# A fused attention and expert block on one Trainium2 core: set-up, the last batch's gathers and the experts' gathers put in another order

## The chip, the cores and the metric

The kernel runs on one core of a Trainium2 chip. A core has five engines, each with its own queue: TensorE (PE, matrix products into PSUM), VectorE (DVE), ScalarE (ACT), GpSimd (POOL) and SyncE (SP, which here only issues DMAs). They wait for each other by semaphores. The metric is the device time of one execution in microseconds; lower is better. All arithmetic is in float32.

## The reference, cut to what matters

```python
mod = (silu(c) @ wmod).reshape(16, 6, 1, 256)
sa, ca, ga, sb, cb, gb = six rows of mod         # ga, gb kept away from zero
h = layernorm(x) * (1 + ca) + sa                 # x is 16 x 1024 x 256
x = x + ga * attention(h)                        # layernorm, q k v, rope, 16 heads of 16,
                                                 # causal softmax, out projection, + h
h = layernorm(x) * (1 + cb) + sb
x = x + gb * experts(h)                          # 8 experts, each gathers 512 rows by index,
                                                 # 256 -> 1024 gelu -> 256, weights, scatter-add
```

The indices are drawn at random, so that one row can belong to several experts, or twice to one.

## The kernel before, in words

**Set-up.** The modulation is computed and written to DRAM, tables of rope are turned, and batch 0 is taken up to its q, k and v. `steps_h` (L428) makes the pieces of the two norms of one half of a batch: statistics `x0` to `x3`, `x moments`, `x power`, `x norm`, `scale`, `shift`, then the same for `h`: statistics (L440, VectorE), `h moments` (L445, VectorE), `h power` (L450 to L454, GpSimd), `bias` (L495, GpSimd, which adds the row `bo_bc`), `h norm` (L465, ScalarE), `gate` and `onto` (GpSimd). In set-up `h_of(2, ...)` issues pieces of batch 1's first half, `h_of(0, ...)` and `h_of(1, ...)` those of batch 0.

`output_bias` (L335) adds the layer norm's offset to v's bias, scales `wv_sb`, and multiplies the bias by Wo into the PSUM tile `pbo` (L352). It returns a function, `joins`, that adds `pbo` to `bo_bc` on VectorE (L359).

**Maxima.** For each group of four heads `maxima` (L622) makes ten steps, each with a product of q and k for every head (L640, into one of six PSUM buffers of the pool `ps_s`) and a minimum of the negated, masked product on VectorE (L658 or L662). The four heads lie in four groups of 32 rows of the array. The first group of batch 0 is done in set-up by `own(n)`: four products, then four minima. Behind step n the loop issues `step_v` of token block n - 1 (L573): a product `pv` in the one buffer of the tag `misc`, and ScalarE's copy into `v_pad` (L583).

**Attention.** A batch has four groups of ten steps; a step issues scores `s` (L717), the exponential on ScalarE (L730), GpSimd's triangular mask on diagonal blocks (L735, steps 0, 1, 2, 5, 7 and 9), the products `o` with v (L764) of the step before, and the maxima of the group that follows. Lists name what else each step issues: `pieces` (products), `inside` (VectorE) and `extra` (the rest), all in program order. In the last batch, `extra` holds twenty gathers of modulation rows for experts 0 and 1 (`rows_mod`, L187, issued in L100); output rows of batch 2 are projected (L856), copied by ScalarE (L869) and added to x by GpSimd (`y`, L876), in steps 2 and 4 of groups 1 and 2.

**Experts.** The attended rows lie in DRAM in `rows` and `out`. For expert e: rows are gathered (`rows_x`, tile `xg`), VectorE takes their statistics (`stats`, L1220, L1222), GpSimd the inverse deviation (`powers`, L1226, L1227), VectorE norms and modulates them (`hidden`, L1235 to L1241), TensorE turns them (`turned`, L1250) and makes `ph` (`first`, L1261, with ScalarE's gelu in L1264), `often` (VectorE) counts rows that occur more than once, and `second` makes `fo` (L1286, two PSUM buffers), weighs it (L1289, L1290), adds the current row of `out` (L1294, tile `cur`, gathered by `rows_now`), and scatters the sum back (L1296). Since rows repeat, a scatter waits for the scatter before it, and the gathers of `cur` for the last scatter of the expert before.

**Order.** TensorE, VectorE, ScalarE and GpSimd issue in program order throughout, SP too in set-up; in the rest a scheduler places SP's DMAs. GpSimd issues every gather and scatter, each in one instruction, between its other work.

Of the kernel before, what the change touches and what calls it, by code (L numbers as in the profile page):

```python
# [11 lines left out]
F32 = mybir.dt.float32  # L12
# [4 lines left out]
ALU = mybir.AluOpType  # L17
AX = mybir.AxisListType

P = 128  # L20
# [7 lines left out]
def adaln_block_kernel(  # L28
# [27 lines left out]
    nc = tc.nc  # L56

    B, L, D = x.shape
# [139 lines left out]
    with ExitStack() as actx:  # L198
# [136 lines left out]
        def output_bias():  # L335

            pv = ps_s.tile([P, QC], F32, name="pb_v", tag="s")[:, :KC]
            for j in range(KC):
                for k in range(KC):
                    nc.tensor.matmul(  # L340
                        pv[:, j : j + 1],
                        lhsT=wv_sb[:, k, ts(j, P)],
                        rhs=bet[:, k : k + 1],
                        start=(k == 0),
                        stop=(k == KC - 1),
                    )
            nc.vector.tensor_tensor(bvc, pv, bvc, ALU.add)
            for k in range(KC):
                nc.vector.tensor_scalar(wv_sb[:, k, :], wv_sb[:, k, :], gam[:, k : k + 1], None, ALU.mult)
            pbo = ps_s.tile([P, QC], F32, name="pbo", tag="s")[:, :D]  # L350
            for k in range(KC):
                nc.tensor.matmul(  # L352
                    pbo,
                    lhsT=bvc[:, k : k + 1].to_broadcast([P, P]),
                    rhs=wo_rows[:, k, :],
                    start=(k == 0),
                    stop=(k == KC - 1),
                )
            return lambda: nc.vector.tensor_tensor(bo_bc, pbo, bo_bc, ALU.add)  # L359

        def indices():
            nc.vector.tensor_single_scalar(bidx, idx, shift, ALU.arith_shift_right)
# [578 lines left out]
        def do(items):  # L941
            for item in items:
                (item[1] if isinstance(item, tuple) else item)()

        with tc.manual_schedule(engines=ORDERED | {ET.SP}):
            nc.sync.dma_start(out=c_sb, in_=cT.rearrange("(k p) b -> p k b", p=P))
            load_wm(0)
            load_x(0)
            raw = [spare("rot00", f"raw{n}").rearrange("p (k n) -> p k n", k=KC) for n in range(2)]
            tabs = [  # L950
                spare("rot01", f"tab{n}")[:, : NT * DH].rearrange("p (t d) -> p t d", d=DH) for n in range(2)
            ]
            for n, src in enumerate((rope_cos, rope_sin)):
                nc.scalar.dma_start(out=tabs[n], in_=src)
            for n, src in enumerate((Wq, Wk)):
                nc.scalar.dma_start(out=raw[n], in_=src.rearrange("(k p) n -> p k n", p=P))
            nc.scalar.activation(sg, c_sb, AF.Sigmoid)
            constants()
            for n, src in enumerate((bq, bk)):
                nc.sync.dma_start(out=bcol[:, n, :], in_=src.rearrange("(p e) -> p e", e=2))  # L960
            nc.sync.dma_start(out=gam, in_=ln_gamma)
            nc.sync.dma_start(out=bet, in_=ln_beta)
            load_x(1)
            load_wm(1)
            nc.sync.dma_start(out=wv_sb, in_=Wv.rearrange("(k p) n -> p k n", p=P))
            nc.sync.dma_start(out=idx, in_=top_idx.rearrange("(t p) e -> p t e", p=P))

            for a in range(2):
                for g in range(GH):
                    to = slice(W * g + DH * a, W * g + DH * (a + 1))  # L970
                    at_ = dict(a=2, g=GH, d=DH)
                    nc.sync.dma_start(out=wo_sb[to], in_=Wo.rearrange("(k a g d) n -> a g d k n", **at_)[a, g])
            wo_rows = spare("rot11", "wo_rows").rearrange("p (k n) -> p k n", k=KC)
            nc.sync.dma_start(out=wo_rows, in_=Wo.rearrange("(k p) n -> p k n", p=P))
            nc.sync.dma_start(out=bvc, in_=bv.rearrange("(k p) -> p k", p=P))
            nc.sync.dma_start(out=bo_bc, in_=bo.partition_broadcast(P))
            nc.vector.tensor_mul(sg, sg, c_sb)
            first_rows()
            hs = [steps_h(0, half) for half in range(NC)] + [steps_h(1, 0)]
            turns, turned, rots, vs = prep[0]  # L980

            def h_of(n, *names):
                for name in names:
                    hs[n].pop(name)()


            for half in range(NC):
                tables(half)
                h_of(half, "x0", "x1", "x2", "x3", "x moments", "x power")
            copies = modulation_products(0)  # L990
            for n in range(2):
                for e in range(2):
                    for k in range(KC):
                        nc.vector.tensor_scalar(
                            wqk[:, k, n, e, :], raw[n][:, k, e::2], gam[:, k : k + 1], None, ALU.mult
                        )
            input_bias()
            ones()
            h_of(0, "x norm0", "x norm1")
            h_of(1, "x norm0", "x norm1")  # L1000
            do(copies)
            copies = modulation_products(1)
            h_of(0, "scale0", "scale1", "shift0", "shift1", "h0", "h1", "h2", "h3", "h moments", "h power")
            do(copies)
            h_of(1, "scale0", "scale1")
            h_of(1, "shift0", "shift1", "h0", "h1", "h2", "h3", "h moments", "h power")
            h_of(0, "h norm0", "h norm1")
            do(turns[0])
            modulation(0)
            load_mod(0)  # L1010
            load_mod(1)
            modulation(1)
            h_of(1, "h norm0", "h norm1")
            indices()

            do(turned[0][:4] + rots[0][:1])
            h_of(2, "x0", "x1", "x2", "x3", "x moments", "x power")
            do(turned[0][4:])
            do(turns[1])
            tokens()  # L1020
            joins = output_bias()
            h_of(2, "x norm0", "x norm1")
            do(rots[0][1:])
            operands(0, 0, 0)
            h_of(2, "scale0", "scale1", "shift0")
            do(turned[1][:4] + rots[1][:1])
            h_of(2, "shift1")
            do(turned[1][4:] + rots[1][1:])
            operands(0, 0, 1)
            h_of(2, "h0", "h1", "h2", "h3", "h moments", "h power")  # L1030
            joins()
            units, place = maxima(0, 0)

            def own(n):
                product, rest = units[n]
                tiles = [product(h) for h in range(GH)]
                for h in range(GH):
                    rest(h, tiles[h])

            for n in range(NS):  # L1040
                own(n)
                do(vs[n - 1 : n] if n else [])
                if n == 0:
                    operands(0, 1)
                    h_of(2, "bias0", "bias1", "h norm0", "h norm1")
                if n == mid:
                    place(0)
                if n == mid + 3:
                    h_of(2, "gate0", "gate1", "onto0", "onto1")
                    for half in range(NC):  # L1050
                        h_of(half, "bias0", "bias1", "gate0", "gate1", "onto0", "onto1")
            do(prep[1][0][0])
            place(1)
            load(2)
            assert not any(hs), [h.keys() for h in hs]
        actx.enter_context(tc.manual_schedule(engines=ORDERED))
        for b in range(B):
# [16 lines left out]
            if b + 1 == B:  # L1074
# [1 line left out]
                    each(pw, w[8 * c + 8 : 8 * c + 12])  # L1076
                at(2, [lambda: weights_1(0), first_mod, early_mod])
                at(2 * NS + mid + 4, [lambda: weights_2(0)])
                for n in range(5):
                    for t_ in range(NCT):  # L1080
                        at(NS + n * NCT + t_, [lambda n=n, t_=t_: rows_mod(t_)[n]()])
                at(3 * NS, [gated[b]])
                each(proj[b][0], [at0 + 3 * NS + mid + n for n in range(3, 7)])
            elif b > 0:
# [220 lines left out]

    nc.scalar.activation(fc.tile([P, 1], F32, name="table"), eps[:, 0:1], AF.Gelu_apprx_tanh)

    def later_mod(e):

        m = fw.tile([P, NCT, 3 * D], F32, name=f"modg_{e}", tag="modg", bufs=3)  # L1310
        for t in range(NCT):
            gather(m[:, t, :], mod_c[:, :], bidx[:, t, e : e + 1])
        X[e]["shift"], X[e]["scale"] = m[:, :, 0:D], m[:, :, D : 2 * D]
        X[e]["gate"] = lambda t: m[:, t, 2 * D : 3 * D]

    halves = ALL[: NCT // 2], ALL[NCT // 2 :]
    for at in halves:
        stats(0, at)
        powers(0, at)
        rows_x(1, range(1) if at[0] == 0 else range(1, NCT))  # L1320
    for at in halves:
        hidden(0, at)
        turned(0, at)

# [14 lines left out]
    for e in range(E):  # L1339
# [5 lines left out]
            turned(e + 1)  # L1345
        if e + 2 < E:
            stats(e + 2)
            later_mod(e + 2)
        if e > 0:
            rows_now(e)  # L1350
        if e + 2 < E:
            powers(e + 2)
        if e + 3 < E:
            rows_x(e + 3)
# [74 lines left out]
```

## Time and profile before

| | us |
|---|---|
| median of three runs | 2824.04 (2823.45 to 2824.58) |
| the profiled execution, its own time | 2825.22 |
| its span, first to last instruction | 2823.5 |
| set-up, until the first maxima are done on TensorE | about 76 |
| attention | about 2490 |
| experts | about 255 |

| stretch, us | TensorE busy | VectorE | ScalarE | GpSimd | granted clock |
|---|---|---|---|---|---|
| 0 to 36 | 25.48 | 31.82 | 14.80 | 18.28 | 0.91 |
| 36 to 76 | 37.14 | 33.74 | 8.34 | 38.03 | 0.87 |
| 76 to 2412 | 2334.29 | 1831.72 | 1478.76 | 1331.14 | 1.00 |
| 2412 to 2564 | 146.94 | 88.66 | 92.62 | 69.59 | 1.00 |
| 2564 to 2597 | 18.05 | 16.29 | 6.47 | 20.04 | 0.74 |
| 2597 to 2819 | 214.57 | 115.53 | 38.84 | 105.62 | 0.99 |

Times in the profile are microseconds from the start of the span. A row of an order of time reads: start, duration, engine, line, operation, output<-input, and in brackets how long the engine was idle before it and what ended that. "Granted clock" is the share of TensorE's full clock in the stretch. A product is shown until its modelled end, so a busy TensorE isn't TensorE at its best rate.

### The profile page before, as it was taken

The numbers are of one execution on the slowest core, as the hardware profiler recorded it, in microseconds if no ns is written. First come the engines' busy times: TensorE is split into PE (matmuls) and PEld (weight loads), VectorE is DVE, ScalarE is ACT, GpSimd is POOL, SyncE is SP. The second block draws the span as 40 slices with busy tenths as digits, with TensorE's granted clock in tenths as the row PEclk, the third lists the DMA queues.
The fourth block names the chain that finished last, engine by engine and source line by source line (L and its number), as shares of the span: only waits on it lengthen the run. The fifth ranks groups of instructions, "written<-read, shape, count | busy, mean of one in ns | idle before, by whom it ended". The sixth has DMA issues, their size and how long they took to land.

```text
span 2823.5 us, 63046 instructions
## 1 busy us (share of the span) xinstructions
PE 2776.5 (98%) x22409; PEld 1274.6 (45%) x22409; DVE 2117.8 (75%) x6759; ACT 1639.8 (58%) x3342; POOL 1582.7 (56%) x2187
## 2 busy tenths in 40 slices
PE   8999999999999999999999999999999999997998
PEld 5444444444444444444444444444444444444665
DVE  8887878787878778787878777787878777754554
ACT  3566666666666666666666666666666665662211
POOL 7565655546564655556464646555554666354552
PEclk8999999999999999999999999999999999998999
DMA  4211222212122222222121222222222222124551
GB/s 143 65 45 41 57 54 68 64 51 73 52 62 60 67 60 56 55 69 64 51 71 52 61 64 66 53 58 62 69 62 54 67 48 66 49 78 163 175 198 54
DMA packets 200314, 199.84 MB, mean 71 GB/s; under 512 B 93248, under 2 KB 154368, under 8 KB 200000
## 3 DMA queue, kind: packets, MB, share of 16 engines
q1 hardware_dynamic: 173888, 148.35, 19.7%
q0 software_dynamic: 8448, 24.78, 2.7%
q10 hardware_dynamic: 17664, 22.68, 2.6%
q8 instruction: 177, 2.90, 0.4%
q14 instruction: 137, 1.12, 0.1%
HBM read 118.94 MB, written 75.66 MB: 69 GB/s over the span
## 4 chain that ended last, share of the span: by engine, by line
PE 94%; POOL 1%; DVE 1%; issue 1%; DMA 1%; ACT 0%; POOLq 0%; SPq 0%; DVEq 0%; ACTq 0%
PE s L717 41%; PE o L764 21%; PE pqk L545 9%; PE m L640 6%; PE pv L576 5%; PE pw L856 5%; PE ph L1261 3%; PE fo L1286 3%; PE ptx L526 1%; DMA cur<-out_dram,idx 0%; POOL modg L100 0%; DMA xg<-rows,idx 0%; DVE wide L311 0%; PE fpt L1250 0%; POOL r L495 0%
## 5 line engine op out<-in xcount | busy, mean ns | idle before, releaser
L730 ACT ACTIVATE p<-s 128x512 f32<-128x512 f32 (+1 forms) x2560 | 1279.5, 552 | 882.1 <-PE m L640 814.4
L640 PE MATMUL m<-ko,qo 32*128 32x512 f32 (+3 forms) x6144 | 1407.4, 526 | 1.7 <-DVE bo_bc L359 1.5
L717 PE MATMUL s<-qo,ko 32*128 32x512 f32 (+3 forms) x6144 | 1351.9, 524 | 0.4 <-DMA qo<-max 0.4
L735 POOL TENSOR_SCALAR_AFFINE_SELECT p<-p 128x256 f32<-128x256 f32 x1024 | 417.7, 416 | 937.2 <-ACT p L730 934.2
L658 DVE TENSOR_REDUCE mt<-m 128x1 f32<-128x512 f32 x1024 | 669.6, 685 | 209.3 <-PE m L640 188.4
L717 PEld LDWEIGHTS s<-qo,ko 32*128 32x128 f32 x6144 | 513.0, 183 | 594.4 <-issue 423.9
L764 PE MATMUL o<-p,v_pad 128*32 128x256 f32 (+3 forms) x6848 | 651.4, 463 | 3.2 <-POOL p L735 2.9
L662 DVE CUSTOM_DVE_ANT_0 masked<-m,dmask,mt 128x256 f32<-128x256 f32 (+3 forms) x1024 | 515.3, 546 | 130.3 <-PE m L640 129.2
L662 DVE CUSTOM_DVE_ANT_0 masked<-m,dmask 128x512 f32<-128x512 f32 (+3 forms) x1024 | 454.9, 486 | 194.6 <-PE m L640 170.8
L640 PEld LDWEIGHTS m<-ko,qo 32*128 32x128 f32 x6144 | 561.8, 183 | 10.0 <-DVE mt L662 3.1
L764 PEld LDWEIGHTS o<-p,v_pad 128*32 128x32 f32 x6848 | 149.1, 108 | 427.1 <-issue 173.9
L545 PE MATMUL pqk<-xnT,wqk 128*128 128x256 f32 x1024 | 286.6, 405 | 0.9 <-ACT xnT L527 0.9
L545 PEld LDWEIGHTS pqk<-xnT,wqk 128*128 128x128 f32 x1024 | 175.2, 189 | 190.8 <-issue 148.3
L479 POOL TENSOR_TENSOR h<-h,mod 128x512 f32<-128x512 f32 x120 | 152.7, 1274 | 67.7 <-ACT h L465 64.4
L662 DVE DVE_READ_ACCUMULATOR2_ANT mt<- 128x1 f32 x2048 | 169.7, 83 | 0.0
L576 PE MATMUL pv<-wv_sb,xnT 128*128 128x256 f32 x512 | 146.6, 409 | 0.3 <-ACT v_pad L583 0.3
L1264 ACT ACTIVATE gT<-ph,b_sb 128x512 f32<-128x512 f32 x64 | 43.9, 687 | 177.2 <-PE ph L1261 171.6
L856 PE MATMUL pw<-wo,onT 128*128 128x256 f32 x512 | 144.2, 405 | 0.6 <-DVE onT L813 0.6
L576 PEld LDWEIGHTS pv<-wv_sb,xnT 128*128 128x128 f32 x512 | 87.7, 191 | 97.7 <-issue 68.7
L552 DVE SCALAR_TENSOR_TENSOR rot<-pqk,bcol,cosT 128x256 f32<-128x256 f32 x256 | 122.0, 477 | 8.0 <-PE pqk L545 3.8
L856 PEld LDWEIGHTS pw<-wo,onT 128*128 128x128 f32 x512 | 86.9, 189 | 89.3 <-issue 70.9
L552 DVE SCALAR_TENSOR_TENSOR rot<-pqk,bcol,sinT 128x256 f32<-128x256 f32 x256 | 121.3, 474 | 0.0
(136 smaller groups left out, 2236.3 us busy)
## 6 DMA issues: line engine op xcount, KB each, us to landing
ops<-rot SPq DMA_DIRECT2D x128, 256.0 KB
rec<-rec_d SPq DMA_DIRECT2D x504, 32.0 KB
rows<-y SPq DMA_DIRECT2D x62, 256.0 KB
out_dram<-y SPq DMA_DIRECT2D x62, 256.0 KB
w<-in_W_dram SPq DMA_DIRECT2D x14, 1024.0 KB
qo<-ops SPq DMA_DIRECT2D x192, 64.0 KB
ko<-ops SPq DMA_DIRECT2D x192, 64.0 KB
x<-in_x_dram ACTq DMA_DIRECT2D x24, 512.0 KB
```

The lines of the kernel that those rows point to most:

```text
L479: nc.gpsimd.tensor_tensor(h, h, row(n), op)
L545: nc.tensor.matmul(ps, lhsT=wqk[:, k, n, e, :], rhs=xt[:, k, ts(u, QW)], start=(k == 0), stop=(k == KC - 1))
L552: nc.vector.scalar_tensor_tensor(s["rot", half, n, e, f][:, ts(u, QW)], ps, bcol[:, n, e : e + 1], tab[:, half * QC + u * QW : half * QC + ...
L576: nc.tensor.matmul(pv, lhsT=S[b]["xnT", t // TC][:, k, ts(t % TC, P)], rhs=wv_sb[:, k, :], start=(k == 0), stop=(k == KC - 1),)
L640: nc.tensor.matmul(sc[:, sum(w[:n]) : sum(w[: n + 1])], lhsT=q[rows, ts(i, P)], rhs=k[rows, c * QC : c * QC + w[n]], start=True, stop=True,)
L658: nc.vector.tensor_reduce(dst, sc[:, 0:w], AX.X, ALU.max, negate=True)
L662: nc.vector.tensor_tensor_reduce(out=masked[:, 0:w], in0=sc[:, 0:w], in1=dmask[:, QC - w : QC], scale=-1.0, scalar=mt[half][:, 0, h, i % T ...
L717: nc.tensor.matmul(sc[:, o:e], lhsT=k[rows, ts(j_, P)], rhs=q[rows, c_ * QC + q0 : (c_ + 1) * QC], start=True, stop=True,)
L730: nc.scalar.activation(p[:, h, 0:end], sc[:, 0:end], AF.Exp, scale=scale)
L735: nc.gpsimd.affine_select(out=mine, in_=mine, compare_op=ALU.is_ge, fill=0.0, base=0, pattern=[[0, 3 - n], [0, n], [1, P]], channel_multip ...
L764: nc.tensor.matmul(acc[c][W * g : W * (g + 1), q0:q1], lhsT=v[:, j, h * VW + 1 - DH * (G % 2) : h * VW + 1 - DH * (G % 2) + W], rhs=p[:, g ...
L856: nc.tensor.matmul(po, lhsT=s["onT", c][:, k, ts(t, P)], rhs=s["wo"][:, k, :], start=(k == 0), stop=(k == KC - 1),)
```

## The change

It moves instructions; it adds and removes none.

1. `pbo` and its addition to `bo_bc` become `product_bias`, issued behind step 0 of the maxima. Before, the product stood in `output_bias`, the addition ahead of step 0.
2. The statistics, moments and power of batch 1's `h` move from ahead of step 0 to behind step 2; so do its bias and norm, which stood behind step 0.
3. In `own(n)` the product of v stands between the products of heads 0, 1 and those of heads 2, 3, ahead of the minima.
4. The twenty gathers of `rows_mod` go into steps 3, 6 and 7 of group 0 (two each) and steps 2, 3, 6 and 7 of groups 1 and 2 (one, two, two, two) instead of one in each step of groups 1 and 2.
5. In the loop over experts, the modulation rows of token blocks 0 and 1 are gathered ahead of the current rows, those of blocks 2 and 3 behind them; before, all four stood ahead.
6. In the first expert, `hidden` and `turned` of the first half of the rows come before `stats` of the second half.

```diff
+        def product_bias():
             pbo = ps_s.tile([P, QC], F32, name="pbo", tag="s")[:, :D]
...
-            return lambda: nc.vector.tensor_tensor(bo_bc, pbo, bo_bc, ALU.add)
+            nc.vector.tensor_tensor(bo_bc, pbo, bo_bc, ALU.add)
...
-            joins = output_bias()
+            output_bias()
...
-            h_of(2, "h0", "h1", "h2", "h3", "h moments", "h power")
-            joins()
             units, place = maxima(0, 0)
 
             def own(n):
                 product, rest = units[n]
-                tiles = [product(h) for h in range(GH)]
+                tiles = [product(h) for h in range(GH // 2)]
+                do(vs[n - 1 : n] if n else [])
+                tiles += [product(h) for h in range(GH // 2, GH)]
                 for h in range(GH):
                     rest(h, tiles[h])
 
             for n in range(NS):
                 own(n)
-                do(vs[n - 1 : n] if n else [])
                 if n == 0:
+                    product_bias()
                     operands(0, 1)
+                if n == mid - 1:
+                    h_of(2, "h0", "h1", "h2", "h3", "h moments", "h power")
                     h_of(2, "bias0", "bias1", "h norm0", "h norm1")
...
-                for n in range(5):
-                    for t_ in range(NCT):
-                        at(NS + n * NCT + t_, [lambda n=n, t_=t_: rows_mod(t_)[n]()])
+
+                free = steps([(3, 3, 6, 6, 7, 7), (2, 3, 3, 6, 6, 7, 7), (2, 3, 3, 6, 6, 7, 7)])
+                for i, n in enumerate(free):
+                    at(n, [lambda i=i: rows_mod(i % NCT)[i // NCT]()])
...
-    def later_mod(e):
-
-        m = fw.tile([P, NCT, 3 * D], F32, name=f"modg_{e}", tag="modg", bufs=3)
-        for t in range(NCT):
+    def later_mod(e, at):
+
+        if at[0] == 0:
+            X[e]["mod"] = fw.tile([P, NCT, 3 * D], F32, name=f"modg_{e}", tag="modg", bufs=3)
+        m = X[e]["mod"]
+        for t in at:
             gather(m[:, t, :], mod_c[:, :], bidx[:, t, e : e + 1])
...
         rows_x(1, range(1) if at[0] == 0 else range(1, NCT))
-    for at in halves:
         hidden(0, at)
         turned(0, at)
...
         if e + 2 < E:
             stats(e + 2)
-            later_mod(e + 2)
+            later_mod(e + 2, halves[0])
         if e > 0:
             rows_now(e)
         if e + 2 < E:
+            later_mod(e + 2, halves[1])
             powers(e + 2)
```

## The prediction

> **What bounds the kernel now.** I read the engines' shares first, then the chain that ended last, then TensorE's waits.
>
> ```profile
> PE 2776.5 (98%) x22409; PEld 1274.6 (45%) x22409; DVE 2117.8 (75%) x6759; ACT 1639.8 (58%) x3342; POOL 1582.7 (56%) x2187
> ...
> PE 94%; POOL 1%; DVE 1%; issue 1%; DMA 1%; ACT 0%; POOLq 0%; SPq 0%; DVEq 0%; ACTq 0%
> ```
>
> TensorE is the bound over attention, whose order the diff leaves alone. The edits can only touch the places where TensorE stands idle or slow. Its waits (total, times, longest) name them:
>
> ```profile
> PE fpt L1250 <- issue: 13.6, 1, 13.6
> PE o L764 <- POOL p L735: 2.9, 4, 1.6
> PE fo L1286 <- DVE fy L1289: 2.4, 1, 2.4
> PE m L640 <- DVE bo_bc L359: 1.5, 1, 1.5
> PE fo L1286 <- DVE fy L1294: 0.9, 1, 0.9
> ```
>
> A wait can cost more than itself. The stretches of set-up show the granted clock (the share before "DMA share"):
>
> ```profile
> 47.00:50.00 3.00, 1.54 (x13) 1.15 (x10) 2.40 (x11) 0.00 (x0) 3.00 (x4) 1.00 0.65 175
> 50.00:54.00 4.00, 4.00 (x15) 3.41 (x16) 4.00 (x21) 0.00 (x0) 3.77 (x6) 0.52 0.56 153
> 54.00:57.00 3.00, 2.73 (x12) 0.93 (x11) 1.13 (x9) 2.44 (x5) 3.00 (x4) 0.50 0.25 77
> 57.00:60.00 3.00, 3.00 (x12) 1.41 (x12) 1.47 (x8) 0.38 (x1) 3.00 (x3) 0.50 0.40 101
> ```
>
> After the 1.46 us wait TensorE ran at half clock from 50 to 60, and VectorE stood idle for 1.9 and 2.2 us there.
>
> GpSimd's order of time at a group boundary of the last batch, and VectorE's in two experts:
>
> ```profile
> 2508.34 1.28 POOL L876 TENSOR_TENSOR y<-y,x 128x512 f32<-128x512 f32 x1 [5.78 <-ACT y L869]
> 2509.77 0.96 POOL L100 DMA_INDIRECT gate<-mod_g,bidx  x1
> 2510.75 1.28 POOL L832 TENSOR_TENSOR part<-oT,rec 128x512 f32<-128x512 f32 x1
> 2512.11 1.27 POOL L835 TENSOR_TENSOR onT<-onT,part 128x512 f32<-128x512 f32 x1
> 2513.33 1.51 POOL L735 TENSOR_SCALAR_AFFINE_SELECT p<-p 128x256 f32<-128x256 f32 x4
> ```
>
> ```profile
> 2721.60 0.43 DVE L1294 TENSOR_TENSOR fy<-fy,cur 128x256 f32<-128x256 f32 x1 [5.98 <-DMA cur<-out_dram,idx]
> ...
> 2752.72 0.42 DVE L1294 TENSOR_TENSOR fy<-fy,cur 128x256 f32<-128x256 f32 x1 [7.54 <-DMA cur<-out_dram,idx]
> ```
>
> First, a gather stands between GpSimd's late `y` and the masks that `o` waits for. Second, VectorE waits 5.98 and 7.54 us for current rows.
>
> **The Trainium skill.** "TensorE: Matmul & The Clock Gate", Part 1: the array falls to half rate after about one idle window of 3.4 us, which runs free, and returns after a busy one. The trace agrees on the size (half clock in multiples of about 3.4 us), but a 1.46 us wait was enough. Same page, specification table: only weight loads are pulled ahead; ScalarE, VectorE and GpSimd are strict FIFO. So one product waiting for its PSUM buffer holds all behind it: the trace has this at 50.0. "DMA: Bandwidth & Descriptors", Anatomy of one DMA: about 2 us fixed, mostly the receipt; here a scatter of rows takes 2.41.
>
> **Set-up.** The statistics of batch 1's `h` (L440, L445) and the sum into `bo_bc` leave VectorE's queue ahead of the maxima; `pbo` moves behind the first step; the v projections stand between heads 0,1 and 2,3. SP's order is unchanged.
>
> *Gain.* Without `pbo` (1.10) ahead of pqk, VectorE's wait of 1.58 at 40.43 goes and its rotations end at about 45.75 instead of 47.35. But the first maxima products need q and k loads, issued on SP at 41.86 to 45.97 behind GpSimd's rotation of 38.39 to 41.2, which does not move; so they stay at 46.7 to 47.5. VectorE starts on them at 47.2 instead of 49.86. The split of heads costs TensorE nothing: heads 2,3 of one step run beside heads 0,1 of the next (two passes of 0.53), so a step needs 1.06 plus 1.06 for pv, under VectorE's 2.4 to 2.7.
>
> *New wait.* VectorE: step 0 is 4 x 0.61 to 49.65, `bo_bc` 0.3, step 1 4 x 0.56 and step 2 4 x 0.48 to about 55.3 (with short waits for products), then statistics 4 x 0.36 and 0.34: 57.1. Before, they ended at 49.6. GpSimd, idle from 51.0, starts its power then (1.86, from 50.98 to 52.84): 59.0; two biases of 1.23: 61.4; ScalarE's norm of the second half 1.1: about 62.6; and only then, in its queue, the copy of the third pv (0.37): 63.0. The fourth pv has one PSUM buffer and waits for that copy, and the products of step 4 and on stand behind it. TensorE reaches it near 56.7. It idles 6.4 us, where before the like wait was 0.27 (at 56.73). VectorE eats its six tiles by 60.8 and idles too. From pv3 on, VectorE has 1.2 + 2.7 + 2.4 + 2.7 + 2.4 + 2.15 from about 65, to 78.9; TensorE ends 2.4 ahead of it, at 76.5 instead of 75.5: 1.0 lost. Half clock after 6.4 idle holds for 3.4 to 6.8 us of work, half of that lost: 1.7 to 3.4, say 2.5. TensorE also idles 44.6 to 46.65 before the first products; one slow window there delays step 0 and `pbo` by about 1.3. Sum: 4.8 lost, between 1.0 (no slow clock) and 6.5. GpSimd's remaining 16 operations of 1.23 end at 81 to 82.5 instead of 74.9; the first mask stands 4.2 behind TensorE's end (79.76 against 75.52), so near 84.5: covered, but by 2 only.
>
> **Gathers of the last batch.** Twenty gathers (0.95 and 0.30 of issue each) move from one a step to free steps without masks. At the boundaries of groups 1 and 2 none stands behind the late `y` any more; masks come 0.96 + 0.15 = 1.1 earlier, twice: 2.2 gained (at 2474.99 `o` took 1.70 instead of 0.64 with a wait of 0.25, so there is that much to gain at each). In the new places: after step 3's none, GpSimd then waits for `rec` until 2431.6; after steps 6 and 7 of group 0, 2.5 us each inside idle stretches of 4.89 and 1.06 + 2.10; the last pushes `onT` (2446.45) to 2447.8, done before its mask at 2449.82. Cost nothing, 0.7 to spare. Range 1.5 to 2.7.
>
> **Experts.** Two of four modulation gathers (1.26 each) go behind the four of the current rows. Current rows are asked for 2.5 earlier and queue behind half the modulation's bytes. TensorE has two `fo` buffers of 3.45 us each, so VectorE may wait about 5.1 before TensorE does: 5.98 gave 0.87, 7.54 gave 2.43. Against this, at 2710.72 and 2740.29 the last scatter was issued just as a weight load of 1 MB began (SP, 2710.34 and 2739.90); scatters issued so late in other experts held the next for 5.4 to 6.5 instead of 3.2. So the gather may start not 2.5 but 1 to 2 earlier; it then finds an emptier queue, lands in about 2.5 to 3 instead of 4.5 and 6.0, and VectorE's waits become about 3. Both TensorE waits go, 3.3, and the slow clock after the second (16 products in 5.37 instead of 3.47): 1.9. Sum 5.2, between 3.3 and 5.5. GpSimd's later half of the modulation is needed an expert later: hidden.
>
> **First expert.** `hidden` of the first half (0.70 + 0.69 + 0.74) now precedes the second half's statistics. The first starts 1.1 earlier (2573.55 against 2574.68), but nothing uses it alone. The second: statistics from 2575.7, VectorE done at 2576.7, GpSimd's power to 2577.9, `hidden` to 2580.2 instead of 2579.04. All hidden rows are needed for `ph` (2580.32), and ScalarE's eight DMA issues to 2585.26 start behind the copies, so `ph` and its activation come 1.1 later: 1.25 lost with the slow clock, 0 to 2.
>
> **Sum** on the profiled execution (span 2823.5; own time 2825.22, 1.2 above the median 2824.04): +4.8 - 2.2 - 5.2 + 1.25 = -1.35. The median becomes 2822.7.
>
> **Rivals.** (1) The set-up's stall meets no slow clock, as the free window allows: 1.0 instead of 4.8, in all -5.2: 2818.9. For: before had phases of full clock beside waits of 0.9. Against: 6.4 idle is near two windows. (2) Slower: in experts 4 and 5 the current rows' gather waits for the last scatter, held by the weights until they are in, as issues 2738 on suggest. If it lands later than 5.1 after VectorE is ready, TensorE still waits and the 5.2 shrink to nothing: +3.9, 2827.9. For: the coincidence within 0.4 us in both experts. Against: once the scatter lands, only two modulation gathers are ahead. (3) The norm's detour is hidden after all, and set-up wins what VectorE stops idling, 3.7: 2814.2. Against: ScalarE's order is fixed.
>
> **Numbers.** Forecast 0.50 (alone 2820 to 2825.5), rival 1 0.22, rival 2 0.20, rival 3 0.05, worse 0.03. Leaving a tenth at each side and adding the bounds: 2818.0 to 2828.2. A change of 0.2% is 5.65 us, about what a measurement can tell: faster takes rival 3 and a third of rival 1, 0.12; slower the tail of rival 2 and worse, 0.06; within 0.82.
>
> **What would show it.** A TensorE wait of some 6 us at `pv` for ScalarE's `v_pad` near 57 to 63, slow clock after; no wait at `fo`; `o` at group boundaries without gather ahead; VectorE's `cur` waits under 5; `ph` of the first expert about 1 later. Wrong if pv does not wait, or `fo` still does.

## The result, and the profile after

The changed kernel takes 2830.47 us (median of 14 runs, 2825.33 to 2836.7) against 2822.93 (14 runs, 2819.03 to 2824.69): 1.0029 times the time, 95% interval 1.0022 to 1.0036. It is slower by 7.5 us by the medians. The forecast was 2822.7, and 2828.2 its upper end. The profiled execution has a span of 2829.1 us (its own time 2831.12), 5.6 more than the one before. The profiles hold less of the loss than the medians, since the profiled execution of before lay 2.3 above the median of its 14 runs, that of after 0.7.

TensorE is still the bound. From the page of the kernel after, its engines and its chain:

```profile
PE 2778.5 (98%) x22409; PEld 1276.1 (45%) x22409; DVE 2118.3 (75%) x6759; ACT 1639.6 (58%) x3342; POOL 1585.6 (56%) x2187
...
PE 95%; DVE 1%; DMA 1%; POOL 1%; issue 1%; ACT 0%; POOLq 0%; ACTq 0%; DVEq 0%; SPq 0%
```

Where the 5.6 us lie comes out of the starts and ends of named products in the two traces:

| stretch, us | before | after | difference | forecast |
|---|---|---|---|---|
| start to the first `s` | 76.11 | 82.98 | +6.87 | +4.8 |
| to the end of the last `pv` | 2341.24 | 2340.95 | -0.29 | 0 |
| to the end of the last `s` | 135.72 | 133.22 | -2.50 | -2.2 |
| to the first `fo` | 44.25 | 45.77 | +1.52 | +1.25 |
| to the end of the last `fo` | 217.54 | 217.56 | +0.02 | -5.2 |
| to the end | 8.60 | 8.61 | 0 | 0 |

TensorE's waits after (us in total, times, longest):

```profile
PE pv L578 <- ACT v_pad L585: 6.0, 1, 6.0
...
PE fo L1291 <- DVE fy L1294: 3.5, 1, 3.5
PE fpt L1255 <- DVE hn L1246: 3.1, 1, 3.1
...
PE o L766 <- POOL p L737: 1.5, 3, 0.6
PE m L642 <- DMA ko<-ops: 1.4, 1, 1.4
```

Two rows answer to the forecast as it had them: the wait at `pv` is there, and the longest wait of `o` fell from 1.6 to 0.6. The `fo` row doesn't: there were 3.3 us in two waits before, and there are 3.5 in one now.

Set-up after, in order of time, all engines:

```profile
57.30 0.38 ACT L585 COPY v_pad<-pv 128x256 f32<-128x256 f32 x1 [2.10 <-PE pv L578]
...
59.25 1.40 DVE L442 BATCH_NORM_STATS2 st_h<-h 128x6 f32<-128x256 f32 x4
...
61.01 0.20 POOL L452 TENSOR_TENSOR rstd_h<-mv_h,eps 128x4 f32<-128x4 f32 x1 [9.35 <-DVE mv_h L447]
...
64.13 2.31 ACT L467 ACTIVATE h<-h,nmr_h,rstd_h 128x256 f32<-128x256 f32 x4 [6.46 <-POOL r L497]
66.35 0.35 ACT L585 COPY v_pad<-pv 128x256 f32<-128x256 f32 x1
...
66.75 0.80 PE L578 MATMUL pv<-wv_sb,xnT 128*128 128x256 f32 x1 [6.02 <-ACT v_pad L585]
```

This is the detour, one engine after another: VectorE's statistics at 59.25, GpSimd idle for 9.35 until they are there, ScalarE idle for 6.46 until GpSimd's bias is there, then the norm, and only behind it the copy that empties the buffer of `pv`. The third `pv` was done at 59.7; its copy took 0.35 and came 6.7 later.

Last comes GpSimd's order at a group boundary of the last batch, where a gather stood second before:

```profile
2513.68 1.27 POOL L878 TENSOR_TENSOR y<-y,x 128x512 f32<-128x512 f32 x1 [4.51 <-ACT y L871]
2514.91 1.28 POOL L834 TENSOR_TENSOR part<-oT,rec 128x512 f32<-128x512 f32 x1
...
2517.49 1.51 POOL L737 TENSOR_SCALAR_AFFINE_SELECT p<-p 128x256 f32<-128x256 f32 x4
```

### The profile page after: what moved, and what is told of

It is laid out like the page before. It is cut to its first block, busy times and chain, and to the rows that moved or that the text cites. A ratio compares the mean times of both kernels' runs of the same rounds, so it can differ in the third digit from the quotient of the medians.

```text
span 2829.1 us, 63049 instructions
## 1 busy us (share of the span) xinstructions
PE 2778.5 (98%) x22409; PEld 1276.1 (45%) x22409; DVE 2118.3 (75%) x6759; ACT 1639.6 (58%) x3342; POOL 1585.6 (56%) x2187
## 4 chain that ended last, share of the span: by engine, by line
PE 95%; DVE 1%; DMA 1%; POOL 1%; issue 1%; ACT 0%; POOLq 0%; ACTq 0%; DVEq 0%; SPq 0%
PE s L719 41%; PE o L766 21%; PE pqk L547 9%; PE m L642 6%; PE pv L578 5%; PE pw L858 5%; PE ph L1266 4%; PE fo L1291 4%; PE ptx L528 1%; PE fpt L1255 0%; DMA out_dram<-fy,idx 0%; ACT p L732 0%; DVE wide L311 0%; POOL r L497 0%; DVE rot L554 0%
```

## The theory tried, and its rival

In the experts the forecast held that what counts is when the current rows are asked for. A rival comes from the profile after, the **loop theory**: GpSimd goes a **round** per expert (eight gathers of modulation and current rows, the power, four gathers of rows, four scatters, each of which waits for the one before). Before, from the first scatter of one expert to that of the next, the rounds are 29.39, 31.23, 30.18 and 30.75; after, 29.22, 31.94, 32.31 and 31.57. TensorE needs 28.4. So, by this theory, GpSimd falls behind TensorE by 2 to 3 us an expert on average until TensorE waits, and moving a gather within the round shortens nothing. All engines after, from the last scatters of the fifth expert to the current rows of the sixth:

```profile
2744.35 0.37 SPq L155 DMA_DIRECT2D w<-in_W_dram  x1
2744.36 0.97 POOL L1301 DMA_INDIRECT out_dram<-fy,idx  x1 [2.22 <-issue]
...
2750.82 0.97 POOL L1301 DMA_INDIRECT out_dram<-fy,idx  x1 [5.49 <-issue]
...
2753.39 0.96 POOL L100 DMA_INDIRECT modg<-mod_c,bidx  x1 [0.30 <-issue]
2754.72 0.95 POOL L100 DMA_INDIRECT cur<-out_dram,idx  x1 [0.37 <-DMA out_dram<-fy,idx]
...
2758.29 0.43 DVE L1299 TENSOR_TENSOR fy<-fy,cur 128x256 f32<-128x256 f32 x1 [8.66 <-DMA cur<-out_dram,idx]
...
2759.11 0.71 PE L1291 MATMUL fo<-w,gT 128*128 128x256 f32 x1 [3.55 <-DVE fy L1294]
```

The third scatter was issued in the same moment as a weight load (SP's row); the fourth had to wait 5.49 instead of 2.2. Only two gathers stand ahead of the current rows, and still VectorE waited 8.66 for them and TensorE 3.55.

## Experiments: each part alone

**Set-up alone** (parts 1 to 3).

```diff
                 if n == 0:
+                    product_bias()
                     operands(0, 1)
+                if n == mid - 1:
+                    h_of(2, "h0", "h1", "h2", "h3", "h moments", "h power")
                     h_of(2, "bias0", "bias1", "h norm0", "h norm1")
...
```

> Before, with the set-up part of the change alone. The forecast: 4.8 us slower than before (between 1.0 and 6.5). The profile of the changed kernel, where the first score product came 6.9 us later (82.98 against 76.11): 6 to 7 us slower, with one TensorE wait of about 6 us at a pv for ScalarE's v_pad. Rival: 1.15 of these 6.9 us is the slow clock's phase near 30 us, ahead of anything that was moved, and belongs to the execution; then about 5.7 us slower.

Measured: 2827.78 against 2821.24, 1.0027 (1.0017 to 1.0038), slower by 6.5 us by the medians. The first `s` starts at 83.71, with one wait of 6.1 at `pv` for `v_pad`. So this part alone is most of the loss. Its expert code is that of before, and there was no wait at `fo` at all in this execution: 212.21 us from the first `fo` to the last instead of 217.54. The interval can't tell the rival of the clock's phase apart, but the profile speaks against it: up to the transposes `ptx` at 36.24 the slow clock had cost 0.6 more than before, not 1.15, and the first `s` came 7.6 later all the same.

**Gathers of the last batch alone** (part 4).

```diff
-                for n in range(5):
-                    for t_ in range(NCT):
-                        at(NS + n * NCT + t_, [lambda n=n, t_=t_: rows_mod(t_)[n]()])
+
+                free = steps([(3, 3, 6, 6, 7, 7), (2, 3, 3, 6, 6, 7, 7), (2, 3, 3, 6, 6, 7, 7)])
+                for i, n in enumerate(free):
+                    at(n, [lambda i=i: rows_mod(i % NCT)[i // NCT]()])
```

> Before, with the last batch's gathers in the free steps alone. The forecast: 2.2 us faster (1.5 to 2.7), the waits of o for masks at the boundaries of groups 1 and 2 gone. Rival: the gathers delay something else and the gain is under 1 us.

Measured, against the same 2821.24: 2818.64, 0.9991 (0.9984 to 0.9998), faster by 2.6 us by the medians; last `pv` to last `s` takes 133.17. This is as forecast, at the upper end of its range.

**Split of the modulation's gathers alone** (part 5).

```diff
...
-            later_mod(e + 2)
+            later_mod(e + 2, halves[0])
         if e > 0:
             rows_now(e)
         if e + 2 < E:
+            later_mod(e + 2, halves[1])
```

> Before, with the split of the modulation's gathers alone. The forecast: 5.2 us faster (3.3 to 5.5), no wait at fo. Loop theory (GpSimd's round of gathers and scatters takes 30 to 31 us an expert, longer than TensorE's 28.4; the split moves the current rows forward within the round but shortens nothing, and where a scatter is held it adds GpSimd's own wait for it): 0 to 1.5 us faster, the last expert's fo still waits 2 to 4 us, and rounds are 1 to 2 us longer where a gather of current rows waits for the scatter.

Measured: 2819.66, 0.9999 (0.999 to 1.0007). A gain of 3.3 or more is outside the interval. In the profiled execution there is one wait at `fo`, of 0.8, less than the 2 to 4 of the loop theory, and the experts take 213.09. That is inside what the code of before shows in other executions (212.21 and 214.93 in the two runs above).

**First expert's order alone** (part 6).

```diff
         rows_x(1, range(1) if at[0] == 0 else range(1, NCT))
-    for at in halves:
         hidden(0, at)
```

> Before, with the first expert's order alone. The forecast: 1.25 us slower (0 to 2). From the profile of the changed kernel: 1.5 us slower. Phase theory: it also shifts TensorE's weight loads and GpSimd's scatters against each other by about 1.5 us, so that the waits at fo change by another -2 to +2 us.

Measured: 2822.0, 1.0003 (0.9994 to 1.0012); last `s` to first `fo` 44.84 instead of 44.25, with the wait of `fpt` for the second half's `hn` at 3.1 instead of 1.1. The time can't tell this from nothing.

The four ratios multiply to 1.0020, where the whole change has 1.0029. With intervals of about 0.001 to either side of each, this leaves open whether the parts also act on each other.

## Experiments: the set-up

**The norm behind the copies.** In the changed kernel, ScalarE's norm goes five steps on, from behind step 2 to behind step 7 (there are ten, and `NS - 3` is 7; the expectation says three); the statistics stay late.

```diff
-                    h_of(2, "bias0", "bias1", "h norm0", "h norm1")
+                    h_of(2, "bias0", "bias1")
+                if n == NS - 3:
+                    h_of(2, "h norm0", "h norm1")
```

> The changed kernel with one thing moved: batch 1's norm of h on ScalarE stands three steps later, behind the v_pad copy of the step before the last two, statistics and biases stay where the change put them. If the stall is the copy behind the norm (the forecast's mechanism): no wait at pv, TensorE ahead of VectorE's maxima again, first score product at 75 to 77 instead of 83, whole kernel 6 to 8 us faster than the changed one, so 2820 to 2823 beside 2821 before. Rival: the stall only moves (pv waits elsewhere, or VectorE or the first ptx waits for the late norm) and the gain is under 3 us.

Measured: 2825.59 against 2820.58, 1.0021 (1.0013 to 1.0028). The wait at `pv` is gone and the first `s` starts at 76.36, so the copy behind the norm was what stalled TensorE. But by the medians the kernel is still 5.0 us slower than before. Its interval overlaps that of the whole change, so how much of the time came back is not settled. GpSimd and TensorE of this kernel a little later:

```profile
82.57 2.47 POOL L501 TENSOR_TENSOR x<-x,r 128x512 f32<-128x512 f32 x2
85.00 1.16 POOL L737 TENSOR_SCALAR_AFFINE_SELECT p<-p 128x256 f32<-128x256 f32 x3
...
85.47 1.07 PE L766 MATMUL o<-p,v_pad 128*32 128x256 f32 x6 [2.77 <-POOL p L737]
```

GpSimd, which starts its set-up work 10 us late, still does it when the first masks are due; `o` waits 2.77. The next view of this kernel has the rest of the price. After the stretch's length come the busy times of TensorE, its weight loads, VectorE, ScalarE and GpSimd, then the granted clock, the DMA share and GB/s:

```profile
84.00:88.00 4.00, 2.53 (x20) 1.42 (x24) 0.00 (x0) 0.00 (x0) 2.52 (x5) 0.50 0.89 290
88.00:92.00 4.00, 4.00 (x36) 1.94 (x32) 2.48 (x12) 1.75 (x4) 1.18 (x3) 0.75 0.77 267
```

From the first `s` to the last `pv` it takes 2346.18 instead of 2341.24. In these two profiles the late statistics are paid either at `pv` or at the mask. That all of the price here comes from the mask is not shown; the next kernel bears on it.

**The statistics back where they were**, the rest of the set-up's change kept.

```diff
+            h_of(2, "h0", "h1", "h2", "h3", "h moments", "h power")
             units, place = maxima(0, 0)
...
                     product_bias()
                     operands(0, 1)
-                if n == mid - 1:
-                    h_of(2, "h0", "h1", "h2", "h3", "h moments", "h power")
                     h_of(2, "bias0", "bias1", "h norm0", "h norm1")
```

> Before, with the set-up part but for batch 1's statistics, biases and norm, which stay where the kernel before has them (ahead of the maxima, after the first step): what moves is the product for the output's bias and v's projections between the heads. If the statistics' move is the cause of the set-up's loss: no wait of 6 us at pv, GpSimd's set-up ends near 75 as before, and the 7 us are gone: between 4 us faster (VectorE starts on the maxima 1.6 earlier, the wait at m and its slow clock go) and 1 us slower. Rival, the split of heads or the product behind step 0 costs as well: 2 to 7 us slower than before.

Measured: 2827.47 against 2828.66, 0.9998 (0.9991 to 1.0005). So the loss is the move of the statistics with what hangs on them; the product of the output's bias and the split of heads cost nothing and bring nothing that can be measured. The 4 us of gain did not come: the first product of the maxima waits 1.7 for the last rotation, and the half clock is there all the same (0.50 from 50 to 60). The profiled execution, 5.3 above the median of this kernel, has half clock later too:

```profile
80.00:84.00 4.00, 4.00 (x18) 2.02 (x20) 1.81 (x9) 2.42 (x4) 0.27 (x1) 0.61 0.04 6
```

TensorE had no wait in the 20 us ahead of this, and no mask was late. The kernel lost some 3 us here against the one before, so in the kernel with the late norm, too, part of the slow clock may have another cause than the mask; what set it off is open.

## Experiments: the experts

**Current rows ahead of all the modulation's**, in the kernel before.

```diff
-            later_mod(e + 2)
         if e > 0:
             rows_now(e)
+        if e + 2 < E:
+            later_mod(e + 2)
```

> Before, with the current rows' gathers ahead of all four of the modulation, a double dose of the changed kernel's edit. The forecast's theory: current rows 5 us earlier, no fo wait: 2 to 5 us faster than before. Loop theory: GpSimd then waits itself for the last scatter to land, 2 us or more in each expert and 4 to 6 where it is held, its round grows from 30 to 31 to 31 to 33, and the late experts wait at fo all the same: between 1 us faster and 3 us slower.

Measured, against 2820.58: 2826.52, 1.0023 (1.0014 to 1.0032), slower by 5.9 us by the medians, more than either theory said. GpSimd in the sixth expert:

```profile
2746.58 0.97 POOL L1296 DMA_INDIRECT out_dram<-fy,idx  x1 [3.35 <-DVE fy L1290]
2751.14 0.99 POOL L100 DMA_INDIRECT cur<-out_dram,idx  x1 [3.59 <-DMA out_dram<-fy,idx]
```

The gather that was to come early waits for the last scatter itself, and with it everything behind it in GpSimd's queue: 1.7 to 3.6 in every expert from the second on. The four gathers of the modulation had covered that wait.

**Rows' gathers between the scatters**, in the kernel before.

```diff
                 in_=y[:, t, :],
                 in_offset=None,
             )
+            if e + 3 < E:
+                rows_x(e + 3, [t])
...
-        if e + 3 < E:
-            rows_x(e + 3)
         second(e)
```

> Before, with the four gathers of rows for the expert after next but one (5.0 us of GpSimd) put between its four scatters, where it waits 2.2 us each for the scatter before. Loop theory: GpSimd's round falls from 30 to 31 by about 3 to 5 us and is then TensorE's 28.4; VectorE's waits for current rows stay under 4 us in every expert, no fo wait; 2 to 5 us faster than before (5.3 is what the profiled execution of before has in fo waits and slow clock; its other executions are shorter). Theory of the forecast (what counts is only how early the current rows are asked for beside the modulation): current rows come no earlier by this within a round, so no difference.

Measured, against the same 2820.58: 2818.96, 0.9996 (0.9987 to 1.0005). GpSimd in the fifth expert:

```profile
2716.01 1.06 POOL L1296 DMA_INDIRECT out_dram<-fy,idx  x1 [1.90 <-DVE fy L1294]
2717.38 0.98 POOL L100 DMA_INDIRECT xg<-rows,idx  x1 [0.30 <-issue]
2719.29 1.00 POOL L1296 DMA_INDIRECT out_dram<-fy,idx  x1 [0.93 <-DVE fy L1294]
```

A gather now fills the time in which GpSimd waited for a scatter. VectorE waits for current rows in no expert, TensorE nowhere at `fo`; the products of one expert begin 28.42 to 28.43 after those of the one before. GpSimd is now early enough that, in the first five experts, a weight load meets only the last of the four scatters. That scatter still lands late (issued at 2725.76, landed at 2730.73), but four gathers of modulation stand between it and the first request that needs it. So the edit does two things at once: it fills GpSimd's waits, and it takes the scatters out of the loads' way. No run parts the two. In the time the gain is 1.6 by the medians, and the interval reaches past none.

**Without the weights of experts 4 to 7** (they use those of experts 2 and 3), in the kernel before.

```diff
-            weights_1(e + 2)
-            weights_2(e + 2)
+            if e < 2:
+                weights_1(e + 2)
+                weights_2(e + 2)
+            else:
+                X[e + 2]["w1"], X[e + 2]["w2"] = X[e]["w1"], X[e]["w2"]
```

> Before, with the weights of experts 4 to 7 left out: these experts use those of experts 2 and 3 again (eight loads of 1 MB less). If the weight loads hold the scatters (next scatter 4 to 6 us later instead of 2.2 of waiting): from expert 3 on all four scatters follow one another in 3.2, rounds fall to 27 to 28.4, no fo wait, 2 to 5 us faster. Rival: the scatters are held by something else (the rows' gathers on the same queue) and the waits of 4 to 6 stay.

Measured, against 2820.58: 2818.76, 0.9993 (0.9983 to 1.0002), which does not tell it from before. There is no wait at `fo`. The longest wait between two scatters of an expert, from the third on, was 4.4, 5.3 and 4.4 before and is 2.3, 3.9 and 2.9 now. So the loads hold the scatters, but not they alone. What holds the rest is not shown; the first scatter stands behind four gathers of rows on the same queue. Rounds of 28.8 and 29.7 were above what was expected.

**The changed kernel without the split.**

```diff
-            later_mod(e + 2, halves[0])
+            later_mod(e + 2)
         if e > 0:
             rows_now(e)
         if e + 2 < E:
-            later_mod(e + 2, halves[1])
```

> The changed kernel with the split of the modulation's gathers undone, the rest of the change kept. Loop theory: the split is worth little either way also here, experts of 212 to 217.6 from the first fo to the last, against 217.56; whole kernel 5 to 9 us slower than before, as with the split. The forecast's theory: without the split 3 to 5 us more, so 11 to 13 us slower than before. Rival, the split is itself a part of the loss in this kernel: 2 to 5 us slower than before.

Measured: 2827.59 against 2822.38, 1.0019 (1.0012 to 1.0026), experts of 213.56. So the split shows no gain in this kernel; whether it costs nothing or some 3 us stays open, since the two intervals (this one and 1.0022 to 1.0036) overlap a little.

The mean of the first four rounds and the experts' stretch, over these profiles:

| kernel | mean round, us | first `fo` to last, us | waits at `fo` of 0.5 or more, us |
|---|---|---|---|
| rows' gathers between the scatters | 28.57 | 212.06 | none |
| set-up alone | 29.35 | 212.21 | none |
| no loads for experts 4 to 7 | 29.81 | 212.06 | none |
| after, without the split | 29.83 | 213.56 | 0.8 |
| last batch's gathers alone | 30.38 | 214.93 | 0.6, 1.7 |
| before | 30.39 | 217.54 | 0.9, 2.4 |
| first expert's order alone | 30.49 | 214.07 | 0.6, 0.9 |
| split alone | 30.79 | 213.09 | 0.8 |
| after | 31.26 | 217.56 | 3.5 |
| after, norm behind the copies | 31.37 | 216.51 | 2.8 |
| current rows first | 32.55 | 221.36 | 2.4, 3.0 |

In the main, the longer the round, the longer the experts, with a spread of some 4 us where it is 30 to 31. A round and a wait of TensorE can each lengthen the other, so the table alone doesn't say which is the cause; the two kernels whose edits lengthen and shorten the round, current rows first and rows' gathers between the scatters, speak for the round. One profile doesn't fit: with the statistics back, 29.85 and 217.51. There VectorE's first `fy` of an expert, not the current rows, comes late (4.1 of waiting in the fourth expert), and the trace doesn't name what it waits for; that is left open.

## Experiments: the parts that gain, together

**Last batch's gathers in free steps, rows' gathers between the scatters**: these two edits from above, in the kernel before.

```diff
+                free = steps([(3, 3, 6, 6, 7, 7), (2, 3, 3, 6, 6, 7, 7), (2, 3, 3, 6, 6, 7, 7)])
...
+            if e + 3 < E:
+                rows_x(e + 3, [t])
...
```

> Before, with the last batch's gathers in the free steps and the rows' gathers between the scatters, nothing of the set-up, the first expert and the modulation's split. If the two gains add: 2.5 (0.9991 alone) and 1.6 to 3 (0.9996 alone, experts of 212.06 instead of 212 to 217.5): 4 to 5.5 us faster than before, ratio 0.998 to 0.9986. Rival, they share one gain: 2.5 us or less.

Measured: 2819.69 against 2828.66, 0.9973 (0.9962 to 0.9983). So the two do not share one gain. The ratio is better than what the parts give together, 0.9987. The mean round is 28.58, and the experts take 212.06 again; before itself was 6 to 8 us longer on this chip than in the other comparisons, and its expert code took 217.51 there in the profile with the statistics back. So there was probably more to gain in the experts here, but no profile of before on this chip shows it.

**The same with the set-up's harmless parts.**

```diff
...
+                tiles = [product(h) for h in range(GH // 2)]
+                do(vs[n - 1 : n] if n else [])
+                tiles += [product(h) for h in range(GH // 2, GH)]
...
+                    product_bias()
...
```

> The set-up with the statistics where they were, the last batch's gathers in the free steps, and the rows' gathers between the scatters. Sum of its parts: 4 to 5.5 us from the last two, and -1 to 4 from the first: 3 to 9 us faster than before. If the set-up without the statistics' move costs time after all, it is slower than the kernel with the two others alone by that much.

Measured, against the same 2828.66: 2820.67, 0.9978 (0.9969 to 0.9988). Nothing is added. The kernel with the two parts is faster than the one before by 0.27%; by the ratios it is faster than the changed one as well, which did not run beside it.

## Why the prediction was wrong

**Set-up: mechanism right, size off.** The chain from the statistics to the copy is as it was written. That the wait is 6.02 where 6.4 was said is in part luck: TensorE reached it at 60.7 instead of 56.7, and the copy ended at 66.7 instead of 63.0. Mis-sized is the term "step 1 and step 2 to about 55.3 (with short waits for products)". VectorE began on the maxima at 48.24 instead of 47.2, and where the term leaves about 1.2 for waits, VectorE waited 0.47, 1.15 and 2.21 for products of a TensorE at half clock, 3.8 together. The longest of these is where a `pv`, 2.08 us at half clock, now stands between the heads. So the statistics ended at 60.9 instead of 57.1, and the copy came 3.7 late, for which the forecast had 1.3, its slow window. From the copy to the last product of the maxima it took 15.7 us instead of 13.5 (63.0 to 76.5), 2.2 for which it had put 2.5. Together that is 2.1 more than the 4.8, so 6.9. (Its sum for VectorE, 13.55 us from about 65, ends at 78.6 and not at 78.9, which changes little.) The windows of the kernel after, with the granted clock ahead of the DMA share:

```profile
50.00:54.00 4.00, 4.00 (x14) 2.69 (x14) 2.38 (x13) 0.00 (x0) 1.66 (x2) 0.50 0.55 151
...
60.00:64.00 4.00, 0.73 (x8) 0.00 (x0) 4.00 (x13) 0.00 (x0) 2.76 (x5) 0.84 0.23 69
64.00:68.00 4.00, 1.25 (x3) 1.07 (x4) 0.58 (x1) 2.44 (x5) 4.00 (x5) 0.50 0.39 90
68.00:72.00 4.00, 4.00 (x17) 2.38 (x17) 1.14 (x2) 0.37 (x1) 4.00 (x4) 0.50 0.21 53
```

As an estimate from these windows, about 6.8 and 6.2 us of work ran at half clock, so 6.5 were lost, against 10.0 and 5.0 before: the slow clock took 1.5 more, where the forecast counted 3.8. TensorE's waits between 46 us and the first `s` grew by 5.4 (1.36 and 6.02 against 0.28, 1.46 and 0.27). Rival 1 (no slow clock) and rival 3 (hidden) are out. "Covered, but by 2 only" for GpSimd's masks was a warning that the late norm made true.

The forecast's reading of the scatters before, "5.4 to 6.5 instead of 3.2" where they met a load, leaves out the longest of that trace, 7.1.

**Last batch's gathers: right**, 2.50 in the profile and 2.6 alone, for 2.2.

**Experts: the step that failed** is "Both TensorE waits go, 3.3, and the slow clock after the second". The experts took 217.56 for 217.54, with one wait of 3.55 at `fo`. The step's reasoning, that VectorE's waits become about 3, held in the third to fifth expert: 2.63, 2.32 and 4.35 where they were 3.69, 4.15 and 5.98. In the sixth it was 8.66 where it was 7.54. Its bound held, too: 8.66 less TensorE's 3.55 are the 5.1 that VectorE may wait. What it left out is that GpSimd's round is longer than TensorE's, so that what a request gains by going earlier within it is given back. The gather of current rows now waits for the scatter itself, 1.36 in the fourth expert and 1.80 in the fifth, and from the scatter that it waits for to the next one it takes 1.0 and 2.4 longer than before (these rounds are 2.1 and 0.8 longer; the rest is how scatters met loads). Rival 2 had the cause (a scatter beside a weight load) and the size, 0 for 5.2, but not the place. It expected the gather to wait at the last scatter; that came in the fourth and fifth expert, where TensorE didn't wait for it. Where TensorE waited, in the sixth, it was the third scatter of the fifth that had met the load: counted from the first `fo`, that scatter was issued 1.7 later than before and the load 1.1 earlier.

A second fault lies under it. The 5.2 us were what one profiled execution held. Other executions of the same expert code show 212.21 and 214.93 for its 217.54, so a full cure is probably worth less than 5.2 in the median, and 1.6 by the medians was measured for the edit that took the waits away, with an interval that reaches past none.

**First expert: right in kind**, 1.52 in the profile for 1.25, 0.6 in the profile of that part alone.

**The sum.** -1.35 became +5.6 in the profile: 5.2 of the difference from the experts, 2.1 from the set-up. The range missed because its upper end took rival 2 with the set-up's middle value. Both at their bad ends, -2.2 + 6.5 + 1.25 + 0, are 5.6 and 2829.6. The measured median is 0.9 above even that. The two profiles don't show where this last part lies.

## What to carry to other kernels

Before a request is moved forward within an in-order queue, measure that queue's round against the bound engine's: if it is the longer one, look first for something to take out of it or for waits to fill, for a request that used to wait behind other work may now make everything behind it wait. Of the edits to GpSimd's order here, only the one that fills its waits rid TensorE of its own; moving requests forward gave nothing that could be measured, or cost 5.9 us. When a piece of work is moved back, follow its result through every queue that holds something else behind it; curing the first stall only shows the next. And a wait that one execution shows is to be looked for in a second one before its whole length is booked as a gain.

## What was not expected of the hardware

The Trainium skill, "DMA: Bandwidth & Descriptors", Queues, rings and completion order, says that each DMA engine takes turns between queues packet by packet. No view here shows the turns, and they did not keep small transfers from being held: before and after, where a scatter was issued between 0.2 us ahead of a weight load of 1 MB and 1.2 us behind it, GpSimd waited 4.4 to 6.1 us before the expert's next scatter instead of 2.2. Where the loads were left out, the longest such wait was 3.9. Probably that is why the experts' time depends on how scatters and loads happen to fall, by 5 us between executions of one expert code; no run varies this alone.

The same skill's "TensorE: Matmul & The Clock Gate", Part 1, says that the clock's window runs free. The trace agrees in so far as half clock did not begin with the waits: after, it began at about 49.0, 1.9 us behind the end of a wait of only 1.36, and lasted 6.8 us; before, it began at 50.1 and lasted 10.2. With the statistics back, it began at about 79.7 with no wait of TensorE since 58.0; no run shows what set it off.
